# Expert rows of four graphs fetched together, x loaded twice, and upper products in pairs

## The chip, the cores and the metric

The kernel runs on one core of one Trainium2 chip. The metric is device time in microseconds (us) from start to end of the kernel, the median of three timed runs; a profiled run gives the trace beside it. The engines are TensorE (PE, with its weight loads as PEld), VectorE (DVE), ScalarE (ACT), GpSimd (POOL), and SyncE (SP), which here only issues transfers.

## The reference

There are 128 graphs of 128 nodes with 1024 features. A graph-attention layer is followed by a feed-forward layer that adds two of eight low-rank experts per graph. Cut to what matters:

```python
x = x + gnn(layernorm(x), adj, adj, W, a)       # x: (128, 128, 1024) float32
x = x + ffn(layernorm(x), router_w, lora_down, lora_up)

def gnn(h, adj, adj_weight, W, a):              # 16 heads of 64 features
    Wh = (h @ W) split into heads               # (B, 16, N, 64)
    e = leaky_relu(Wh @ a[:F] + Wh @ a[F:], 0.2)
    att = softmax(where(adj == 0, -9e15, e)) * adj_weight
    return elu(att @ Wh), heads joined again

def ffn(x, router_w, lora_down, lora_up):       # 8 experts of rank 16, top 2
    gates = softmax over the two highest of x[:, 0] @ router_w.T
    down = einsum('blh,erh->bler', x, lora_down)
    return x + einsum('bler,ehr,be->blh', down, lora_up, gates)
```

## The kernel before

The kernel walks over pairs of graphs: step q projects graphs 2q and 2q+1 with W (seven products, after Strassen's scheme, of 16 matmuls each), while attention, normalisation and the experts of earlier graphs are placed in the gaps between the products. `gaps[k]` holds what is emitted ahead of product k; every engine works through its own instructions in the order in which they are emitted. A group g is four graphs, two pairs. Its experts are chosen and their rows fetched in step 2g+2 (called an even step below) and used in step 2g+3 (an odd step). `fetch` gathers the down rows with eight indirect transfers that GpSimd issues; `fetch_up` gathers, for one graph, the 128 rows of the two chosen upper matrices (512 KB). The pool `work` has two buffers per tag unless `bufs` says otherwise; `ps_m` has four PSUM buffers of one bank.

The parts that the change and the prediction touch:

```python
    def load_x(q):
        for i in (2 * q, 2 * q + 1):
            X[i] = work.tile([P, D], F32, tag="x", name="xn", bufs=10)
            nc.sync.dma_start(X[i], x[i])

    def load_xt(q):
        XT[q] = work.tile([P, 2, KC, P], F32, tag="xt", name="xt")
        for t in range(2):
            nc.sync.dma_start(XT[q][:, t], x_t[2 * q + t])
# ... cut ...
    def stats(i, mv):

        st = small.tile([P, NH, 6], F32, tag="stats", name="stats")
        for h in range(NH):
            nc.vector.bn_stats(st[:, h, :], X[i][:, h * HALF:(h + 1) * HALF])
        nc.vector.bn_aggr(mv[:, i % 2], st)
# ... cut ...
    def pair_sums(q):

        xt = XT[q]
        a11, a12 = xt[:, 0, 0:KH], xt[:, 0, KH:KC]
        a21, a22 = xt[:, 1, 0:KH], xt[:, 1, KH:KC]
        s1, s2, s4 = (work.tile([P, KH, P], F32, tag=n, name=n, bufs=b)
                      for n, b in (("s1", 1), ("s2", 1), ("s4", 2)))
        nc.gpsimd.tensor_tensor(s1, a21, a22, ALU.add)
        nc.gpsimd.tensor_tensor(s2, s1, a11, ALU.subtract)
        s3 = a21 if q else first_s3
        nc.gpsimd.tensor_tensor(s3, a11, a21, ALU.subtract)
        nc.gpsimd.tensor_tensor(s4, a12, s2, ALU.subtract)
        SUMS[q] = (s1, s2, s3, s4)
# ... cut ...
# project(q), after setup: seven products of 16 matmuls; `bank()` gives 2 PSUM banks, two such buffers
        def product(dst, first, lhs, rhs, half_way=None):
            order = [(j, k) for j in range(2) for k in range(KH)]
            if q == 0:
                order.sort(key=lambda at: at[1])
            for at, (j, k) in enumerate(order):
                if half_way and at == KH:
                    half_way()
                nc.tensor.matmul(dst[:, j, cols], lhs[:, k, :], w_sb[:, rhs, k, j, cols],
                                 start=(first and k == 0), stop=(k == KH - 1),
                                 skip_group_check=not first)

        def read(dst, src, plus):
            nc.vector.tensor_tensor(dst[:, :, cols], src[:, :, cols], plus[:, :, cols], ALU.add)
# ... cut ...
        for step in ((product_1, product_6, product_2, product_5, product_7, product_3, product_4)
                     if q else
                     (product_1, product_2, product_7, product_6, product_5, product_3, product_4)):
            step()
            yield
# ... cut ...
    def update(i):


        att = ATT[i // 2]
        xt = X[i]
        hp = work.tile([P, D], F32, tag="hp", name="hp")
        for h, ph in enumerate(PH.pop(i)):
            nc.vector.tensor_tensor(
                hp[:, h * HALF:(h + 1) * HALF].rearrange("p (h f) -> p h f", f=F),
                ph.rearrange("p (h f) -> p h f", f=F),
                att[:, i % 2, h * HPH:(h + 1) * HPH, None].to_broadcast([P, HPH, F]),
                ALU.mult,
            )
        ex = work.tile([P, D], F32, tag="ex", name="ex", bufs=1)
        nc.scalar.activation(ex, hp, AF.Exp)
        nc.vector.scalar_tensor_tensor(xt, hp, 0.0, xt, op0=ALU.max, op1=ALU.add)
        q, t = divmod(i, 2)
        if t == 0:

            ACC[q] = small.tile([P, 3, 2], F32, tag="acc", name="acc", bufs=2)
        acc = ACC[q][:, :, t:t + 1]
        nc.vector.scalar_tensor_tensor(xt, ex, 1.0, xt, op0=ALU.min, op1=ALU.add,
                                       accum_out=acc[:, 0])
        nc.gpsimd.tensor_scalar(acc[:, 1], acc[:, 0], -1.0 / D, None, op0=ALU.mult)

    def squares(i):

        acc, t = ACC[i // 2], i % 2
        unread = scratch if i < 2 else work.tile([P, D], F8, tag="dn", name="unread", bufs=1)
        nc.scalar.activation(unread, X[i], AF.Square, bias=acc[:, 1, t:t + 1],
                             accum_out=acc[:, 2, t:t + 1], saturate=None if i < 2 else False)
# ... cut ...
    def join(i):

        g, t = divmod(i, G)
        nc.scalar.activation(X[i], X[i], AF.Identity, bias=GRP[g]["off"][:, t:t + 1],
                             scale=GRP[g]["mul"][:, t:t + 1])
# ... cut ...
        at_up = st["at_up"] = small.tile([P, G], U32, tag="at_up", name="at_up", bufs=2)
        nc.vector.tensor_scalar(at_up, of_slot, float(-R), up_row, op0=ALU.mult, op1=ALU.add)
        st["down"] = work.tile([P, G * TOP * R, KC], F32, tag="down", name="down", bufs=1)
        for j in range(G * TOP):
            nc.gpsimd.indirect_dma_start(
                out=st["down"][:, j * R:(j + 1) * R].rearrange("p r k -> p (r k)"), out_offset=None, in_=table,
                in_offset=bass.IndirectOffsetOnAxis(ap=at_down[:, j:j + 1], axis=0))

    def fetch_up(g, t):

        st = GRP[g]
        st["up", t] = work.tile([P, D], F32R, tag="up", name="up")
        nc.gpsimd.indirect_dma_start(
            out=st["up", t].bitcast(F32), out_offset=None, in_=up_table,
            in_offset=bass.IndirectOffsetOnAxis(ap=st["at_up"][:, t:t + 1], axis=0))
# ... cut ...
    def ffn_down(g):

        st = GRP[g]
        pd = ps_m.tile([P, HALF], F32, tag="pm", name="pd")
        # ... 64 matmuls into pd ...
        dn = st["dn"] = work.tile([P, G + 2, P], F32R, tag="ex", name="dn", bufs=1)
        whole = dn[:, G:G + 2]
        nc.scalar.mul(whole[:, 0], pd[:, 0:P], st["gate"])
        nc.vector.scalar_tensor_tensor(whole[:, 1], pd[:, 0:P], st["gate"],
                                       whole[:, 0].bitcast(F32), op0=ALU.mult, op1=ALU.subtract)
        for t in range(G):
            for s in range(G):
                (nc.vector.tensor_copy if s // 2 else nc.scalar.copy)(
                    dn[s * GR:(s + 1) * GR, t], whole[t * GR:(t + 1) * GR, s // 2])

    def ffn_up(g, t):

        st = GRP[g]
        st["pu", t] = [ps_m.tile([P, HALF], F32, tag="pm", name="pu") for _ in range(NH)]
        for h, pu in enumerate(st["pu", t]):
            nc.tensor.matmul(pu, st["dn"][:, t], st["up", t][:, h * HALF:(h + 1) * HALF],
                             start=True, stop=True)

    def add_up(g, t):

        st = GRP[g]
        y = X.pop(g * G + t)
        for h, pu in enumerate(st.pop(("pu", t))):
            cols = slice(h * HALF, (h + 1) * HALF)
            nc.vector.scalar_tensor_tensor(y[:, cols], pu, st["rstd"][:, t:t + 1], y[:, cols],
                                           op0=ALU.mult, op1=ALU.add)
        nc.sync.dma_start(out[g * G + t], y)
# ... cut ...
    NQ = B // 2


    for q in range(NQ + 2):
        gaps = [[] for _ in range(8)]
    # ...
        if ffn and not part:
            gaps[6] += [(logits, g), (choose, g)]
            if g < NG - 1:
                gaps[6] += [(fetch, g), (fetch_up, g, 0), (fetch_up, g, 1)]
        if q < NQ:
            gaps[6] += [(high, q, 3), (high, q, 1)]
            gaps[7].append((high, q, 2))
        # ...
        if 0 < q <= NQ:
            i = 2 * q - 2
            gaps[0].append((attention_weights, q - 1))
            if q > 3 and q % 2 == 0:
                gaps[0] += [(add_up, (q - 4) // 2, 2), (add_up, (q - 4) // 2, 3)]
            gaps[1] += [(attend, i), (update, i)]
            gaps[2].append((attend, i + 1))
            if q < NQ:
                gaps[2] += [(turn, i), (update, i + 1), (squares, i)]
                gaps[3].append((turn, i + 1))
                gaps[4 if ffn and part else 3] += [(squares, i + 1), (second_stats, q - 1)]
                gaps[4].append((rejoin, i))
                gaps[5].append((rejoin, i + 1))
            else:
                gaps[2] += [(squares, i), (update, i + 1), (turn_at_end, i),
                            (keep_turned, i)]
        # ... (last step cut)
            gaps[5 if q < NQ else 7] += [(join, i), (join, i + 1)]
            if i < B - G:
                gaps[1].append((first_row, i))
                gaps[2].append((first_row, i + 1))
        if q + 1 < NQ:
            if q:
                gaps[3].append((first_stats, 2 * q + 2))
            gaps[4 if q and not part else 5].append((pair_sums, q + 1))
            if q:
                gaps[4].append((first_stats, 2 * q + 3))
        # ...
        elif ffn and part:
            gaps[0].append((weigh, g))
            gaps[4].insert(0, (ffn_down, g))
            gaps[5][0:0] = [(ffn_up, g, 0), (ffn_up, g, 1), (add_up, g, 0), (add_up, g, 1),
                            (fetch_up, g, 2), (fetch_up, g, 3)]
            gaps[7] += [(ffn_up, g, 2), (ffn_up, g, 3)]
        # ...
        if q < NQ:
            if q:
                gaps[3].insert(0, (low, q, 0))
            gaps[6 if q else 7] += [(low, q, 3), (low, q, 1)]

        if q + 1 < NQ:
            load_xt(q + 1)
            load_x(q + 1)
        # ...
        products = project(q) if q < NQ else iter(())
        for gap in gaps:
            for f, *args in gap:
                f(*args)
            next(products, None)
```

## Time and profile before

| | before |
|---|---|
| median of three timed runs | 2036.71 us (2035.92 to 2037.42) |
| span of the profiled run | 2057.4 us |
| mean granted PE clock | 0.96 |
| moved by DMA | 380.77 MB, mean 185 GB/s |
| `x` loads | 128 of 512 KB |
| gathers of down rows, of up rows | 248 and 124 |

A line of a view names the line of the kernel, the engine, the operation and the tiles, written tile first and read tiles after the arrow. "Busy" on PE is modelled from pipelined matmuls, so the time that a product takes is read from one start to the next. The granted clock is the share of full speed that the clock of PE was allowed in a stretch.

### The profile page before, as it was taken

What the parts mean: (1) busy time and instruction counts of PE and PEld (TensorE: products, weight loads), DVE (VectorE), ACT (ScalarE), POOL (GpSimd) and SP (SyncE); (2) the same over time, 40 slices, a digit from 0 to 9 for tenths busy, and PEclk for the clock granted to TensorE, in tenths of its full rate; (3) what the DMA queues carried; (4) which work ended last, traced back from release to release, by engine and by line L of the source; (5) the groups of instructions that cost most, each with busy time, mean ns of one, the idle gap of its engine ahead of it and who ended that gap; (6) DMA issues with size and microseconds to landing.
All of it is one profiled execution on the core that took longest, in us unless ns stands there. A gap on an engine that the chain in (4) does not pass through costs nothing.

```text
span 2057.4 us, 29877 instructions
## 1 busy us (share of the span) xinstructions
PE 1937.1 (94%) x10182; PEld 1624.6 (79%) x10182; DVE 1674.0 (81%) x3674; ACT 1292.9 (63%) x1564; POOL 1017.9 (49%) x1388
## 2 busy tenths in 40 slices
PE   9989999999999999999999999999999999999997
PEld 6877877777877788777788777787877788777875
DVE  6878888888887888878888888888888888788876
ACT  3765756657567567566576576675665756666655
POOL 4445544456454465544564544655445545446451
PEclk9999999999999999999999999999999999999998
DMA  8566555666556665666655556656656655566544
GB/s 331 137 196 212 146 181 185 188 205 177 168 188 172 208 196 157 185 166 212 206 172 178 183 172 211 209 144 191 194 178 205 183 165 185 171 211 209 141 146 142
DMA packets 362910, 380.77 MB, mean 185 GB/s; under 512 B 280716, under 2 KB 282892, under 8 KB 362248
## 3 DMA queue, kind: packets, MB, share of 16 engines
q1 hardware_dynamic: 327176, 287.63, 44.9%
q0 software_dynamic: 30400, 89.68, 14.3%
q10 hardware_dynamic: 5184, 1.57, 0.3%
q8 instruction: 81, 1.33, 0.3%
q14 instruction: 69, 0.57, 0.1%
HBM read 243.52 MB, written 69.22 MB: 152 GB/s over the span
## 4 chain that ended last, share of the span: by engine, by line
PE 42%; POOL 16%; DVE 15%; ACT 10%; DMA 9%; issue 8%; DVEq 0%; SPq 0%; POOLq 0%; ACTq 0%
PE pw L472 36%; POOL down L812 10%; DMA up<-up_table,at_up 6%; POOL up L820 4%; PE ph L586 3%; ACT unread L618 3%; DMA down<-table,at_down 3%; DVE wh L477 3%; DVE parts L542 2%; DVE stats L369 2%; ACT y_t L656 2%; DVE dn L844 2%; PE pu L852 2%; ACT dn L844 1%; ACT xn L676 1%
## 5 line engine op out<-in xcount | busy, mean ns | idle before, releaser
L472 PE MATMUL pw<-w_sb,xt 128*128 128x260 f32 (+1 forms) x4080 | 988.0, 399 | 1.0 <-issue 0.8
L472 PEld LDWEIGHTS pw<-w_sb,xt 128*128 128x128 f32 x4080 | 808.2, 199 | 144.2 <-issue 8.2
L472 PE MATMUL pw<-w_sb,s 128*128 128x260 f32 (+1 forms) x3072 | 704.6, 382 | 0.0
L472 PEld LDWEIGHTS pw<-w_sb,s 128*128 128x128 f32 x3072 | 583.0, 190 | 94.3 <-DVE wh L477 0.9
L656 ACT COPY y_t<-tt 128x2048 uint16<-128x2048 uint16 x126 | 309.9, 2492 | 30.8 <-DMA tt<-halves 30.8
L650 ACT COPY halves<-xn 128x2048 uint16<-128x2048 uint16 x126 | 239.9, 1904 | 95.9 <-DVE xn L610 95.9
L812 POOL DMA_INDIRECT down<-table,at_down x248 | 258.5, 1042 | 78.8 <-issue 63.1
L612 POOL TENSOR_SCALAR acc<-acc 128x1 f32<-128x1 f32 x128 | 38.9, 305 | 490.6 <-DVE xn L610 488.2
L542 DVE SCALAR_TENSOR_TENSOR parts<-wh,rstd,parts 128x512 fp32r<-128x512 f32 x192 | 179.4, 961 | 101.7 <-ACT parts L538 101.7
L538 ACT ACTIVATE parts<-wh,rstd 128x512 fp32r<-128x512 f32 x192 | 130.8, 714 | 171.7 <-DVE wh L477 171.7
L603 ACT ACTIVATE ex<-hp 128x1024 f32<-128x1024 f32 x128 | 135.5, 1058 | 140.8 <-DVE hp L596 136.8
L596 DVE TENSOR_TENSOR hp<-ph,att 128x512 f32<-128x512 f32 x256 | 163.9, 682 | 44.2 <-PE ph L586 43.9
L852 PE MATMUL pu<-up,dn 128*128 128x512 f32 x248 | 97.1, 497 | 106.6 <-DMA up<-up_table,at_up 88.6
L630 POOL TENSOR_SCALAR rstd<-acc 128x2 f32<-128x2 f32 x64 | 12.3, 193 | 346.5 <-ACT unread L618 343.5
L618 ACT ACTIVATE unread<-xn,acc 128x1024 fp8e4<-128x1024 f32 x126 | 144.5, 1147 | 53.1 <-POOL acc L612 52.3
L477 DVE TENSOR_TENSOR wh<-pw,p 128x520 f32<-128x520 f32 (+1 forms) x192 | 132.0, 688 | 49.2 <-PE pw L472 46.6
L586 PE MATMUL ph<-parts,adj_f 128*128 128x512 f32 x512 | 165.4, 446 | 4.8 <-DVE xn L861 4.8
L861 DVE SCALAR_TENSOR_TENSOR xn<-pu,rstd,xn 128x512 f32<-128x512 f32 x248 | 168.5, 741 | 0.0
L610 DVE SCALAR_TENSOR_TENSOR xn<-ex,xn 128x1024 f32<-128x1024 f32 x128 | 156.8, 1225 | 13.7 <-ACT ex L603 0.2
L604 DVE SCALAR_TENSOR_TENSOR xn<-hp,xn 128x1024 f32<-128x1024 f32 x128 | 156.8, 1225 | 4.4
L369 DVE BATCH_NORM_STATS2 stats<-xn 128x6 f32<-128x512 f32 x248 | 158.6, 681 | 0.4
L820 POOL DMA_INDIRECT up<-up_table,at_up x124 | 140.5, 1133 | 36.2 <-issue 35.9
(183 smaller groups left out, 1975.8 us busy)
## 6 DMA issues: line engine op xcount, KB each, us to landing
xn<-in_x SPq DMA_DIRECT2D x128, 512.0 KB
xt<-in_x_t SPq DMA_DIRECT2D x127, 512.0 KB
out_y<-xn SPq DMA_DIRECT2D x124, 512.0 KB
adj_f<-in_adj_t POOLq DMA_DIRECT2D x32, 256.0 KB, 3.1
adj_i<-in_adj SPq DMA_DIRECT2D x32, 256.0 KB
down<-table,at_down POOLq DMA_INDIRECT x248, 4.5
w_sb<-in_w SPq DMA_DIRECT2D x3, 1040.0 KB
wt_sb<-in_w_t SPq DMA_DIRECT2D x1, 2048.0 KB
```

Of the source, the lines that this page charges most:

```text
L369: nc.vector.bn_stats(st[:, h, :], X[i][:, h * HALF:(h + 1) * HALF])
L472: nc.tensor.matmul(dst[:, j, cols], lhs[:, k, :], w_sb[:, rhs, k, j, cols], start=(first and k == 0), stop=(k == KH - 1), skip_group_check ...
L477: nc.vector.tensor_tensor(dst[:, :, cols], src[:, :, cols], plus[:, :, cols], ALU.add)
L542: nc.vector.scalar_tensor_tensor(in_two(PARTS[q][:, 1, b]), block, rstd, in_two(PARTS[q][:, 0, b].bitcast(F32)), op0=ALU.mult, op1=ALU.sub ...
L586: nc.tensor.matmul(PH[i][h], GRP[g]["adj_f"][:, t, :], PARTS[q][:, s, NH * (i % 2) + h], start=(s == 0), stop=(s == 1))
L596: nc.vector.tensor_tensor(hp[:, h * HALF:(h + 1) * HALF].rearrange("p (h f) -> p h f", f=F), ph.rearrange("p (h f) -> p h f", f=F), att[:, ...
L618: nc.scalar.activation(unread, X[i], AF.Square, bias=acc[:, 1, t:t + 1], accum_out=acc[:, 2, t:t + 1], saturate=None if i < 2 else False)
L650: nc.scalar.copy(halves, X[i].bitcast(U16).rearrange("p (d s) -> p s d", s=2))
L656: nc.scalar.copy(y_of(i).bitcast(U16).rearrange("p k (n s) -> p s k n", s=2), TT.pop(i).rearrange("p (s k) n -> p s k n", s=2))
L812: nc.gpsimd.indirect_dma_start(out=st["down"][:, j * R:(j + 1) * R].rearrange("p r k -> p (r k)"), out_offset=None, in_=table, in_offset=b ...
L820: nc.gpsimd.indirect_dma_start(out=st["up", t].bitcast(F32), out_offset=None, in_=up_table, in_offset=bass.IndirectOffsetOnAxis(ap=st["at_ ...
L861: nc.vector.scalar_tensor_tensor(y[:, cols], pu, st["rstd"][:, t:t + 1], y[:, cols], op0=ALU.mult, op1=ALU.add)
```

## The change

All four upper gathers of a group are issued in the even step, straight after the eight of the down rows, and land in four buffers of tag `up` where two served before. The room comes from `x`: where a tile of x stayed in SBUF from the statistics (one step ahead) until the expert's output was added, in ten buffers, it is now loaded into one of two buffers of tag `rows` for the statistics and again, late in the step before it is needed, into one of six buffers for the sum. The second pair's upper products and additions follow the first pair's by one product in the same step, where they came at the step's end and in the next step. The joins, which multiply and add the residual on ACT, move to gap 1 of the next step. The small `acc` of each graph moves from GpSimd to DVE. In odd steps the pair sums on GpSimd come one gap earlier and the second statistics one gap later. The aim is that PE doesn't wait for upper rows and that GpSimd's run of gathers holds nobody up.

The diff, with the hunks that only move buffers of the start or rename a list left out:

```diff
--- before.py
+++ after.py
# ... cut ...
@@ -98,9 +98,16 @@
         return t.rearrange("p (j c) -> p j c", j=2)
 
     def load_x(q):
+
         for i in (2 * q, 2 * q + 1):
-            X[i] = work.tile([P, D], F32, tag="x", name="xn", bufs=10)
+            X[i] = work.tile([P, D], F32, tag="x", name="xn", bufs=6)
             nc.sync.dma_start(X[i], x[i])
+
+    def load_rows(q):
+
+        for i in (2 * q, 2 * q + 1):
+            ROWS[i] = work.tile([P, D], F32, tag="rows", name="rows")
+            nc.sync.dma_start(ROWS[i], x[i])
 
     def load_xt(q):
         XT[q] = work.tile([P, 2, KC, P], F32, tag="xt", name="xt")
# ... cut ...
@@ -366,7 +374,7 @@
 
         st = small.tile([P, NH, 6], F32, tag="stats", name="stats")
         for h in range(NH):
-            nc.vector.bn_stats(st[:, h, :], X[i][:, h * HALF:(h + 1) * HALF])
+            nc.vector.bn_stats(st[:, h, :], ROWS[i][:, h * HALF:(h + 1) * HALF])
         nc.vector.bn_aggr(mv[:, i % 2], st)
 
     def rstd_of(dst, var):
@@ -390,7 +398,7 @@
         mv = MV[q][:, t]
         for h in range(NH):
             nc.scalar.activation(scratch[:, h * HALF:(h + 1) * HALF],
-                                 X[i][:, h * HALF:(h + 1) * HALF], AF.Identity,
+                                 ROWS[i][:, h * HALF:(h + 1) * HALF], AF.Identity,
                                  accum_out=mv[:, h:h + 1])
         nc.gpsimd.tensor_tensor(mv[:, 2:3], mv[:, 0:1], mv[:, 1:2], ALU.add)
         nc.gpsimd.tensor_scalar(mv[:, 3:4], mv[:, 2:3], -1.0 / D, None, op0=ALU.mult)
@@ -405,7 +413,7 @@
 
         for t in range(2):
             mv = MV[q][:, t]
-            nc.scalar.activation(scratch, X[2 * q + t], AF.Square, bias=mv[:, 3:4],
+            nc.scalar.activation(scratch, ROWS[2 * q + t], AF.Square, bias=mv[:, 3:4],
                                  accum_out=mv[:, 4:5])
         RSTD[q] = small.tile([P, 2], F32, tag="rstd", name="rstd")
         nc.gpsimd.tensor_scalar(RSTD[q], MV.pop(q)[:, :, 4], 1.0 / D, EPS, op0=ALU.mult,
@@ -609,7 +617,7 @@
         acc = ACC[q][:, :, t:t + 1]
         nc.vector.scalar_tensor_tensor(xt, ex, 1.0, xt, op0=ALU.min, op1=ALU.add,
                                        accum_out=acc[:, 0])
-        nc.gpsimd.tensor_scalar(acc[:, 1], acc[:, 0], -1.0 / D, None, op0=ALU.mult)
+        nc.vector.tensor_scalar(acc[:, 1], acc[:, 0], -1.0 / D, None, op0=ALU.mult)
 
     def squares(i):
 
@@ -805,7 +813,7 @@
         nc.vector.tensor_tensor(mine, chosen, of_two[:, None].to_broadcast([P, G, TOP]), ALU.mult)
         of_slot = small.tile([P, G], F32, tag="of_slot", name="of_slot", bufs=1)
         nc.vector.tensor_reduce(of_slot, mine, AX.X, ALU.add)
-        at_up = st["at_up"] = small.tile([P, G], U32, tag="at_up", name="at_up", bufs=2)
+        at_up = small.tile([P, G], U32, tag="at_up", name="at_up", bufs=2)
         nc.vector.tensor_scalar(at_up, of_slot, float(-R), up_row, op0=ALU.mult, op1=ALU.add)
         st["down"] = work.tile([P, G * TOP * R, KC], F32, tag="down", name="down", bufs=1)
         for j in range(G * TOP):
@@ -813,13 +821,11 @@
                 out=st["down"][:, j * R:(j + 1) * R].rearrange("p r k -> p (r k)"), out_offset=None, in_=table,
                 in_offset=bass.IndirectOffsetOnAxis(ap=at_down[:, j:j + 1], axis=0))
 
-    def fetch_up(g, t):
-
-        st = GRP[g]
-        st["up", t] = work.tile([P, D], F32R, tag="up", name="up")
-        nc.gpsimd.indirect_dma_start(
-            out=st["up", t].bitcast(F32), out_offset=None, in_=up_table,
-            in_offset=bass.IndirectOffsetOnAxis(ap=st["at_up"][:, t:t + 1], axis=0))
+        for t in range(G):
+            st["up", t] = work.tile([P, D], F32R, tag="up", name="up", bufs=4)
+            nc.gpsimd.indirect_dma_start(
+                out=st["up", t].bitcast(F32), out_offset=None, in_=up_table,
+                in_offset=bass.IndirectOffsetOnAxis(ap=at_up[:, t:t + 1], axis=0))
 
     def ffn_down(g):
 
@@ -974,7 +980,7 @@
         if ffn and not part:
             gaps[6] += [(logits, g), (choose, g)]
             if g < NG - 1:
-                gaps[6] += [(fetch, g), (fetch_up, g, 0), (fetch_up, g, 1)]
+                gaps[6].append((fetch, g))
         if q < NQ:
             gaps[6] += [(high, q, 3), (high, q, 1)]
             gaps[7].append((high, q, 2))
@@ -985,14 +991,15 @@
         if 0 < q <= NQ:
             i = 2 * q - 2
             gaps[0].append((attention_weights, q - 1))
-            if q > 3 and q % 2 == 0:
-                gaps[0] += [(add_up, (q - 4) // 2, 2), (add_up, (q - 4) // 2, 3)]
+            if q > 1:
+                gaps[1] += [(join, i - 2), (join, i - 1)]
             gaps[1] += [(attend, i), (update, i)]
             gaps[2].append((attend, i + 1))
             if q < NQ:
                 gaps[2] += [(turn, i), (update, i + 1), (squares, i)]
                 gaps[3].append((turn, i + 1))
-                gaps[4 if ffn and part else 3] += [(squares, i + 1), (second_stats, q - 1)]
+                gaps[4 if ffn and part else 3].append((squares, i + 1))
+                gaps[5 if ffn and part else 3].append((second_stats, q - 1))
                 gaps[4].append((rejoin, i))
                 gaps[5].append((rejoin, i + 1))
             else:
@@ -1001,14 +1008,15 @@
                 gaps[3] += [(squares, i + 1), (turned_parts, NG - 1, False),
                             (turn_at_end, i + 1), (stay_busy, 1, ident), (turned_parts, NG - 1, True),
                             (keep_turned, i + 1), (second_stats, q - 1)]
-            gaps[5 if q < NQ else 7] += [(join, i), (join, i + 1)]
+            if q == NQ:
+                gaps[7] += [(join, i), (join, i + 1)]
             if i < B - G:
                 gaps[1].append((first_row, i))
                 gaps[2].append((first_row, i + 1))
         if q + 1 < NQ:
             if q:
                 gaps[3].append((first_stats, 2 * q + 2))
-            gaps[4 if q and not part else 5].append((pair_sums, q + 1))
+            gaps[4 if q else 5].append((pair_sums, q + 1))
             if q:
                 gaps[4].append((first_stats, 2 * q + 3))
         if ffn and not part:
@@ -1027,9 +1035,8 @@
         elif ffn and part:
             gaps[0].append((weigh, g))
             gaps[4].insert(0, (ffn_down, g))
-            gaps[5][0:0] = [(ffn_up, g, 0), (ffn_up, g, 1), (add_up, g, 0), (add_up, g, 1),
-                            (fetch_up, g, 2), (fetch_up, g, 3)]
-            gaps[7] += [(ffn_up, g, 2), (ffn_up, g, 3)]
+            gaps[5][0:0] = [(ffn_up, g, 0), (ffn_up, g, 1), (add_up, g, 0), (add_up, g, 1)]
+            gaps[6] += [(ffn_up, g, 2), (ffn_up, g, 3), (add_up, g, 2), (add_up, g, 3)]
         if q % 2 == 0 and q < NQ:
             gaps[5].append((group_adj, q // 2))
             if q // 2 + 1 < NG:
@@ -1041,7 +1048,9 @@
 
         if q + 1 < NQ:
             load_xt(q + 1)
-            load_x(q + 1)
+            load_rows(q + 1)
+        if 0 < q < NQ:
+            gaps[6].insert(0, (load_x, q))
         if q == 0:
             gaps[7] += [(sums_of, 2), (sums_of, 3), (load_up,)]
         if q == 1:
```

## The prediction

> **What bounds the kernel now.** I began with the page: busy shares, then the chain that ended last.
>
> ```profile
> PE 1937.1 (94%) x10182; PEld 1624.6 (79%) x10182; DVE 1674.0 (81%) x3674; ACT 1292.9 (63%) x1564; POOL 1017.9 (49%) x1388
> ```
>
> TensorE (PE) is nearly full, so the question is where its missing 6% sits, and whether its "busy" time is all useful. The list of waits, for all engines (us in total, times, longest), answers the first:
>
> ```profile
> ACT parts L538 <- DVE wh L477: 171.7, 64, 3.9
> ...
> PE pu L852 <- DMA up<-up_table,at_up: 88.6, 49, 3.9
> ...
> ACT unread L618 <- POOL acc L612: 52.3, 33, 2.6
> ```
>
> PE has practically one wait, at the upper products of line 852, for the rows being fetched (88.6 us; with other releasers the group's idle time is 106.6 us). The timeline of PE through the end of an odd step shows the pattern:
>
> ```profile
> 945.75 3.67 PE L472 MATMUL pw<-w_sb,s 128*128 128x260 f32 x16
> 949.25 3.67 PE L472 MATMUL pw<-w_sb,xt 128*128 128x260 f32 x16
> 954.56 0.69 PE L852 MATMUL pu<-up,dn 128*128 128x512 f32 x2 [1.64 <-DMA up<-up_table,at_up]
> 956.28 0.71 PE L852 MATMUL pu<-up,dn 128*128 128x512 f32 x2 [1.03 <-DMA up<-up_table,at_up]
> 956.83 5.35 PE L472 MATMUL pw<-w_sb,xt 128*128 128x260 f32 x16
> 961.83 1.28 PE L586 MATMUL ph<-parts,adj_f 128*128 128x512 f32 x4
> ```
>
> Read the starts, not the durations. A product of 16 matmuls takes 949.25 - 945.75 = 3.50 us. The second one should end at 952.75, and four pu matmuls should take 1.12 us (as the first four, 944.63 to 945.75), so the next product should start at 953.87; it starts at 956.83, 2.96 us late. That product then takes 961.83 - 956.83 = 5.00 us where its like in undisturbed steps takes about 3.4: another 1.6. The granted clock in 4 us windows says why (the columns are PE, PEld, DVE, ACT, POOL, then the clock, the DMA share and GB/s):
>
> ```profile
> 948.00:952.00 4.00, 4.00 (x20) 3.48 (x19) 2.16 (x4) 4.00 (x4) 3.51 (x4) 1.00 0.62 188
> 952.00:956.00 4.00, 1.61 (x7) 0.75 (x5) 2.66 (x2) 1.92 (x3) 3.92 (x4) 1.00 1.03 378
> 956.00:960.00 4.00, 3.71 (x11) 3.01 (x12) 3.76 (x14) 0.98 (x2) 1.23 (x1) 0.66 0.99 394
> 960.00:964.00 4.00, 4.00 (x18) 3.35 (x17) 3.69 (x6) 0.59 (x1) 0.00 (x0) 0.91 0.72 297
> ```
>
> The pause costs a second time, by a cold clock. The whole loss is 4.6 us here, 4.7 in the next group; the rest of the group is an unbroken stream of PE work. From 961.83 to the same place in the next group, 1023.78, is 61.95 us; without the loss it is 57.3.
>
> Why the rows are late is in the chain that ended last, in order of time (start, us):
>
> ```profile
> 934.58 0.95 POOL up L820
> ...
> 935.83 1.52 POOL up L820
> ...
> 937.43 0.54 POOL acc L612
> 937.99 1.24 ACT unread L618 x2
> 939.23 0.58 ACT parts L538
> ```
>
> GpSimd (POOL) issues ten gathers in a row, about 1.0 us each and 0.30 us apart, so the small `acc` of line 612 waits behind them, ScalarE (ACT) waits for `acc`, and VectorE (DVE) for ACT. The last two gathers need the two `up` buffers back from the first upper products (945.75); they issue at 948.84 and 950.22 and take a median 6.1 us to land, while PE is ready for them at 952.75.
>
> **What the Trainium skill says.** "TensorE: Matmul & The Clock Gate", Part 1: The HAM clock gate, gives half rate after an idle window of about 3.4 us and full rate only after a busy one. The trace agrees: clock 0.66 in the window after the pause, and 5.00 us for a product. "SBUF — State Buffer", Who interferes with whom: a DVE instruction with two SBUF inputs, or a copy or cast in a two-port mode, shares a port pair with GpSimd, and the second to issue is blocked until the first ends. The trace agrees; the timelines of POOL and of DVE in an even step show it:
>
> ```profile
> 915.28 1.26 POOL L422 TENSOR_TENSOR s<-xt 128x512 f32<-128x512 f32 x1
> ```
> ```profile
> 915.72 0.87 DVE L709 TENSOR_TENSOR add<-of_graph,part 128x32 f32<-128x32 f32 x1
> ```
>
> An operation on 32 elements, which elsewhere takes 0.19 us, ends just as the POOL one does. "DMA: Bandwidth & Descriptors", SWDGE vs HWDGE vs iDMA, says that an engine takes turns between the queues of GpSimd and of SP; this trace does not test it.
>
> **The change part by part.** (1) Gathers of rows 3 and 4 move from the odd step to the even one. Twelve in a row: from 923.82, eight of 1.04 + 0.30 and four of 1.13 + 0.30 make 16.4 us at most, so the last issues at about 939 and lands about 945; needed at 949.25 (the second pair now in gap 6). Their wait goes, and with it the cold product: 31 groups by 4.7 = 145 us, all on the path that sets the end. (2) `acc` on DVE: 128 small instructions at about 0.15 us (the tiny ones of lines 771 and 772), 19 us, 0.6 per group, in exchange for 52.3 us of ACT waiting; beside PE, so it gains nothing by itself but brings ACT's read of product 2 forward by some 1.5 us. (3) Joins, two per step at 1.23 us, go from gap 5 to gap 1 of the next step, where ACT was idle 2.98 us before `ex`; they may delay `ex` by about 0.7. The 2.36 us before lines 538 and 542 in the odd step goes (DVE stood 3.17 us there). (4) x twice: 2.1 MB per group, at the 394 GB/s of a full window 5.4 us of DMA time; DMA goes from 0.60 x 62 = 37 us to 42.6 us of about 58, or 74%. (5) The second x load waits until the first pair's output has left: about 951 to 953, landed by 957, needed about 959.5. It holds, with some 2 us to spare. (6) The upper products of the second pair come one product, not two, after the first, and need the four PSUM buffers that four additions of 0.74 us must free. (7) Pair sums in odd steps move a gap earlier: POOL is then at 5.5 us of additions from about 939.3 to 944.8, just when DVE makes its eight casts into `dn`. These run 0.22 us for 128 elements against 0.19 for 32, so I take them for a two-port mode: each can be blocked by up to 1.3 us. I expect `dn` 1 to 2 us later (0.5 us of waiting at the first pu), then additions ending about 951 with the second pair wanted at 949.9 (0.5 us more). Estimate: 0.8 us x 31 = 25 us given back. These pauses are too short to cool the clock.
>
> Sum in the profile: 2057.4 - 145 = 1912 as floor, +25 = 1937. The timed runs are at 2036.7 while the profiled run took 2059.6. If profiling stretches everything alike, the timed floor is 1912 x 2036.7 / 2059.6 = 1891; if it only lengthens the wait (matmuls should run at their rate either way), it stays 1912. I take the middle, 1902, and add 25: about 1928.
>
> **Rivals.** DVE becomes the bound: it is busy 50.7 us per 62, so 51.3 of 57.3, 90%. For: it is 3 us behind PE in even steps already (`hp` at 929.59 for products begun at 926.63). Against: it still has pauses, 2.03 us at line 542 for ACT, which part 2 shortens. If it bound, gaps would spread: about 1960. The transfers become the bound: twelve gathers, two transposes and the step's loads crowd into 923 to 948, where the share is already 0.85 to 1.02. If transposes land late, ACT's `y_t` waits grow from 30.8 us, and DVE follows: 1950 to 1980. The new x load takes the place of the old wait, if outputs leave late: 2 us and a cold product again, near 2000. Best case, no contention at the casts: 1895 to 1905.
>
> **Range and chances.** 1900 to 1968 covers floor by either reading and all but the last rival. For under 2% the group must keep over 70% of its loss (4.7 less 40.7 / 31 = 1.3 us): faster 0.94, same 0.05, slower 0.01.
>
> **What would show it.** Right: PE's wait for `up` under 10 us, clock 0.99 or 1.00 in the middle windows, period about 58, POOL no longer releasing line 618. Part 7: the DVE casts of line 844 well over 0.22 us, small waits of PE at line 852 for `dn` or line 861. Wrong: PE waiting for `xn` of line 604 or 610 or its DMA, `y_t` waits well over 60 us, or a clock still near 0.96.

## The result, and the profile after

| | before | after |
|---|---|---|
| median of the timed runs | 2037.07 us (2035.92 to 2039.98) | 1982.12 us (1979.68 to 1983.08) |
| span of the profiled run | 2057.4 us | 1980.3 us |
| mean granted PE clock | 0.96 | 0.997 |
| mean period of a group in the trace | 63.1 us | 60.6 us |
| moved by DMA | 380.77 MB | 446.87 MB |

The ratio is 0.9726, 95% interval 0.9709 to 0.9743. The gain is 55 us where 109 were predicted, and the time lies above the predicted range. The period is read from one start of the down products to the next, over 30 groups. The difference, 2.5 us by 30, makes up 75 of the 77 us between the two spans, so the steady groups hold the answer.

The busy shares of the changed kernel, and the first line of its chain that ended last:

```profile
PE 1907.6 (96%) x10182; PEld 1590.9 (80%) x10182; DVE 1689.8 (85%) x3802; ACT 1294.6 (65%) x1564; POOL 944.1 (48%) x1260
...
PE 86%; DVE 5%; issue 3%; DMA 3%; POOL 2%; ACT 1%; another core or an unknown queue 0%; SPq 0%; DVEq 0%; ACTq 0%
```

The chain now runs through PE for 86% of the span, where POOL, DVE, ACT and DMA had half of it before:

```profile
PE 42%; POOL 16%; DVE 15%; ACT 10%; DMA 9%; issue 8%; DVEq 0%; SPq 0%; POOLq 0%; ACTq 0%
```

PE still lacks 4%. Its list of waits (us in total, times, longest) says where:

```profile
PE pd L836 <- issue: 41.9, 57, 1.9
PE pu L858 <- DMA up<-up_table,at_up: 6.3, 3, 3.2
```

The wait for upper rows is down from 88.6 to 6.3 us, as intended. In its place stands a wait that the kernel before did not have, at the down products, with "issue" as releaser: PE waited for nothing that the profile shows. PE's timeline through the end of an odd step of the changed kernel:

```profile
1019.40 3.67 PE L480 MATMUL pw<-w_sb,s 128*128 128x260 f32 x16
1023.00 0.44 PE L836 MATMUL pd<-y_t,down 128*32 128x128 f32 x4
1024.58 0.27 PE L836 MATMUL pd<-y_t,down 128*32 128x128 f32 x1 [1.13 <-issue]
1025.30 1.97 PE L836 MATMUL pd<-y_t,down 128*32 128x128 f32 x59 [0.46 <-issue]
1027.20 3.77 PE L480 MATMUL pw<-w_sb,xt 128*128 128x260 f32 x16
...
1035.25 0.97 PE L858 MATMUL pu<-up,dn 128*128 128x512 f32 x2
1036.43 1.11 PE L858 MATMUL pu<-up,dn 128*128 128x512 f32 x2 [0.21 <-issue]
1037.38 7.17 PE L480 MATMUL pw<-w_sb,xt 128*128 128x260 f32 x32
```

The 64 down products take 4.20 us to the next product (1023.00 to 1027.20). In the kernel before they ran without a gap (939.29 to 941.21, 1.92 us to the next product):

```profile
939.29 1.99 PE L830 MATMUL pd<-y_t,down 128*32 128x128 f32 x64
941.21 3.77 PE L472 MATMUL pw<-w_sb,xt 128*128 128x260 f32 x16
```

From the first start to the last, the trace has 1.71 us in every group before and 3.0 to 4.3 after; the excess over all 31 groups is 65 us, 2.1 per group. The second pair's four upper products take 2.13 us to the next product, which is also the median of 30 groups; a block that nothing holds up took 1.12 (944.63 to 945.75 before). What GpSimd and DVE do meanwhile, in their timelines of the same group:

```profile
1020.84 1.65 POOL L826 DMA_INDIRECT up<-up_table,at_up  x1 [0.30 <-issue]
1022.79 1.02 POOL L826 DMA_INDIRECT up<-up_table,at_up  x1 [0.31 <-issue]
1025.61 1.30 POOL L430 TENSOR_TENSOR s<-xt 128x512 f32<-128x512 f32 x1 [1.79 <-remote]
...
1028.22 1.28 POOL L433 TENSOR_TENSOR xt<-xt 128x512 f32<-128x512 f32 x1
1029.45 1.28 POOL L434 TENSOR_TENSOR s<-xt,s 128x512 f32<-128x512 f32 x1
```
```profile
1029.28 2.97 DVE L850 CAST dn<-dn 32x128 fp32r<-32x128 f32 x8
```

The same casts in the kernel before:

```profile
942.93 1.89 DVE L844 CAST dn<-dn 32x128 fp32r<-32x128 f32 x8
```

Two things coincide. The twelfth gather is being issued until 1023.81, 0.8 us after PE has come to the down products; with ten, the last ended some 2 us ahead of them (935.83 + 1.52 = 937.35, against 939.29). And the pair sums run while DVE makes its casts.

### The profile page after: what moved, and what is told of

The parts are those of the page before. It is cut to its first block, busy times and chain, and to the rows that moved or that the text cites. A ratio compares the mean times of both kernels' runs of the same rounds, so it can differ in the third digit from the quotient of the medians.

```text
span 1980.3 us, 30167 instructions
## 1 busy us (share of the span) xinstructions
PE 1907.6 (96%) x10182; PEld 1590.9 (80%) x10182; DVE 1689.8 (85%) x3802; ACT 1294.6 (65%) x1564; POOL 944.1 (48%) x1260
## 2 busy tenths in 40 slices
DMA packets 381058, 446.87 MB, mean 226 GB/s; under 512 B 282732, under 2 KB 284908, under 8 KB 380392
## 4 chain that ended last, share of the span: by engine, by line
PE 86%; DVE 5%; issue 3%; DMA 3%; POOL 2%; ACT 1%; another core or an unknown queue 0%; SPq 0%; DVEq 0%; ACTq 0%
PE pw L480 73%; PE ph L594 5%; PE pd L836 4%; PE pu L858 3%; DMA up<-up_table,at_up 2%; POOL down L820 1%; DVE xn L867 1%; DMA w_sb<-in_w 1%; DVE wh L485 1%; POOL up L826 0%; DVE parts L550 0%; PE pu L922 0%; DVE hp L604 0%; DVE xn L618 0%
## 5 line engine op out<-in xcount | busy, mean ns | idle before, releaser
L480 PE MATMUL pw<-w_sb,xt 128*128 128x260 f32 (+1 forms) x4080 | 935.5, 385 | 0.5 <-DMA w_sb<-in_w 0.5
L480 PEld LDWEIGHTS pw<-w_sb,xt 128*128 128x128 f32 x4080 | 771.7, 190 | 125.5 <-issue 7.0
L664 ACT COPY y_t<-tt 128x2048 uint16<-128x2048 uint16 x126 | 310.4, 2492 | 54.5 <-DMA tt<-halves 54.3
L546 ACT ACTIVATE parts<-wh,rstd 128x512 fp32r<-128x512 f32 x192 | 136.9, 719 | 227.9 <-DVE wh L485 227.9
L618 DVE SCALAR_TENSOR_TENSOR xn<-ex,xn 128x1024 f32<-128x1024 f32 x128 | 156.8, 1225 | 34.7 <-ACT ex L611 24.6
L377 DVE BATCH_NORM_STATS2 stats<-rows 128x6 f32<-128x512 f32 x248 | 158.6, 681 | 0.4
L826 POOL DMA_INDIRECT up<-up_table,at_up x124 | 135.1, 1089 | 37.8 <-issue 37.2
L684 ACT ACTIVATE xn<-xn,off,mul 128x1024 f32<-128x1024 f32 x128 | 151.8, 1235 | 0.0
L550 DVE SCALAR_TENSOR_TENSOR parts<-wh,rstd,parts 128x512 fp32r<-128x512 f32 x192 | 137.7, 743 | 6.9 <-ACT parts L546 6.8
L836 PE MATMUL pd<-y_t,down 128*32 128x128 f32 x1984 | 84.2, 277 | 42.0 <-issue 41.9
```

Of the source, the lines that this page charges most:

```text
L377: nc.vector.bn_stats(st[:, h, :], ROWS[i][:, h * HALF:(h + 1) * HALF])
L664: nc.scalar.copy(y_of(i).bitcast(U16).rearrange("p k (n s) -> p s k n", s=2), TT.pop(i).rearrange("p (s k) n -> p s k n", s=2))
L836: nc.tensor.matmul(pd[t * GR:(t + 1) * GR, 0:P], st["down"][:, t * GR:(t + 1) * GR, k], st["y_t"][:, k, t * P:(t + 1) * P], start=(k == 0) ...
```

## The experiments

Two theories compete for the down products. **G**: gathers that GpSimd issues as PE comes to them slow PE. **X**: the added load of x, and its traffic, does it. A further question is what the blocked casts cost. The runs used three chips, on which the kernel before took 2042 (e1 to e4), 2062 to 2063 (e5 to e8, e16, e17) and 2047 to 2067 us (e9 to e15), so only runs of one chip, or ratios to the kernel before, are compared. Of each edit the lines that matter are shown. The last column is the time from the first to the last start of the 64 down products, over the first 30 of the 31 groups, worked out from the traces; the last group is told of below the table.

| run | time | ratio to before, 95% interval | down products, us |
|---|---|---|---|
| e1 before, unchanged | 2043.67 | 0.9998 [0.9977, 1.0019] | 1.71 |
| e2 after, two gathers emitted later | 1982.57 | 0.9700 [0.9657, 0.9743] | 3.2 to 5.9 |
| e3 after, second x load cut to 1/16 | 1982.66 | 0.9704 [0.9661, 0.9747] | 3.2 to 4.9 |
| e4 after, pair sums late | 1984.48 | 0.9741 [0.9679, 0.9802] | 3.3 to 5.0 |
| e5 after, two gathers split off | 2002.50 | 0.9698 [0.9663, 0.9732] | 1.71 |
| e6 as e5, other pair sums late | 1913.11 | 0.9262 [0.9208, 0.9316] | 1.71 |
| e7 before, `acc` on DVE | 2006.55 | 0.9730 [0.9703, 0.9756] | 1.71 |
| e8 as e7, three more gathers | 2105.21 | 1.0198 [1.0168, 1.0227] | 4.1 to 6.8 |
| e9 after, again | 1971.47 | 0.9541 [0.9524, 0.9557] | 2.8 to 4.0 |
| e10 e6 again | 1940.16 | 0.9413 [0.9363, 0.9463] | 1.71 |
| e11 after, `acc` on GpSimd | 1968.28 | 0.9526 [0.9510, 0.9542] | 2.6 to 4.1 |
| e12 as e7, GpSimd busy instead | 2019.63 | 0.9868 [0.9820, 0.9916] | 1.71 |
| e13 as e7, three gathers elsewhere | 2017.66 | 0.9864 [0.9816, 0.9911] | 1.71 to 1.74 |
| e14 e7 again | 2013.01 | 0.9843 [0.9788, 0.9898] | 1.71 to 1.80 |
| e15 e8 again | 2126.17 | 1.0382 [1.0328, 1.0437] | 4.9 to 7.2 |
| e16 as e6, one gather split off | 1970.74 | 0.9564 [0.9505, 0.9624] | 1.71 |
| e17 e6 again | 1912.48 | 0.9298 [0.9248, 0.9347] | 1.71 |

The 1913.11 of e6 is the median of three runs; a fourth, 1941.62 at a clock of 0.989, was over 1.5% above the fastest and is left out as disturbed.

The last group of e5, e6, e10, e16 and e17 has no pair sum to hold the late gathers back, so twelve are issued in a row there, the last one until 0.8 us after the first down product in all five. The down products took 2.75, 2.87 and 3.52 us in e5, e6 and e10, but 1.71 in e16 and e17. The part on what stays open comes back to this.

**e1, the kernel before.** Unchanged.

> The kernel before, unchanged, so that its trace comes from the same chip as the others. If the slow start of the down products (their 64 matmuls take 3.0 to 4.3 us from first to last start in the changed kernel, 1.7 us in the trace of the kernel before) belongs to the change, this shows 1.7 us again in every group, PE's semaphore updates on time, and 2035 to 2040 us. If it belongs to the chip or to the way the trace was taken, it shows 3 us or more here too.

It repeats the time of before, and 1.71 us in every group: the slow start belongs to the changed kernel.

**e2, the last two gathers emitted behind the down products.**

```diff
-            gaps[4].insert(0, (ffn_down, g))
+            gaps[4][0:0] = [(ffn_down, g), (fetch_up, g, range(2, 4))]
```

> The changed kernel with its third and fourth gather of upper rows issued in the odd step, just behind the down products, still into four buffers: ten gathers in a row, as before the change. Theory G (the row of twelve gathers, which still runs when PE comes to the down products, slows PE's sequencer there): the down products take 1.7 us again, 65 us go, about 1920 us. Theory X (the second load of x and the traffic it adds): nothing of that moves, 1975 to 1990 us. In both, the late rows must still be there for the second pair: issued about 1026 and 1027 on the clock of the changed kernel's trace, landing about 1033, needed at 1035.

It did not test what it meant to. GpSimd had nothing else to do, so it ran ahead and issued twelve in a row again, from 1014.26 to beyond 1028.71 in one group. The time is that of the changed kernel. Emitting the two gathers behind a PE instruction did not delay them, since GpSimd waited for nothing of PE's there. In two groups of e2 the twelfth gather had ended 0.07 and 0.19 us before the down products began, and they still took 3.2 and 3.3 us.

**e3, the second load of x cut to 64 of its 1024 columns**, into six fixed buffers. The residual sum is left on old contents, so the output is not the reference's.

```diff
-            X[i] = work.tile([P, D], F32, tag="x", name="xn", bufs=6)
-            nc.sync.dma_start(X[i], x[i])
+            X[i] = xbuf[i % 6]
+            nc.sync.dma_start(X[i][:, 0:F], x[i, :, 0:F])
```

> The changed kernel, where the second load of x fetches 64 of 1024 columns only (the sum is then taken over old contents, the work is the same): the traffic that the change added is nearly gone, all instructions stay. Theory X: the down products take 1.7 us, about 1920 us. Theory G: they stay above 3 us and the time is 1970 to 1985 us.

The time did not move, and the wait stayed; from the waits of PE in e3:

```profile
PE pd L840 <- issue: 41.5, 58, 1.9
```

X falls: with 1/16 of the second load nothing changes that these runs can measure.

**e4, pair sums of odd steps back in gap 5.**

```diff
-            gaps[4 if q else 5].append((pair_sums, q + 1))
+            gaps[4 if q and not part else 5].append((pair_sums, q + 1))
```

> The changed kernel with the pair sums of odd steps back in gap 5, behind the eight casts into dn. If the casts are held up by GpSimd's additions, they take 1.9 us again instead of 3.7, the wait of 0.7 us inside the second block of upper products goes, and up to 20 us with it: about 1962 us. If the additions then hold up the low parts of line 550 as much, nothing is gained: 1975 to 1990 us. The down products keep their 3 to 4 us in both.

The casts are free again, in the timeline of DVE in e4:

```profile
731.09 1.89 DVE L850 CAST dn<-dn 32x128 fp32r<-32x128 f32 x8
...
740.88 2.66 DVE L550 SCALAR_TENSOR_TENSOR parts<-wh,rstd,parts 128x512 fp32r<-128x512 f32 x2
```

The second pair's upper products were down to 1.26 us, so the blocked casts were what made them late. But the pair sums now fall on line 550 (2.66 us for two, 0.74 each elsewhere), PE waited 24.0 us for upper rows where it had waited 6.3, and nothing was won. The slow start stayed, so the casts are not its cause.

**e5, the last two gathers put behind the first pair sum**, which overwrites `s1`, a buffer that PE's product ahead of the down products reads, and so can't run ahead.

```diff
         nc.gpsimd.tensor_tensor(s1, a21, a22, ALU.add)
+        if between is not None:
+            fetch_up(between, range(2, 4))
```

> In e2 the two late gathers found GpSimd free and followed the other ten at once, so the row of twelve was not broken. Here they stand behind the first of the pair sums, which waits for PE to finish the product ahead of the down products: ten gathers in a row, ending some 2 us before the down products, then the last two from about 1.5 to 4 us after their start. Theory G (gathers being issued while PE comes to the down products slow its sequencer): the down products take 1.7 to 2 us again and 55 to 65 us go: 1915 to 1930 us. If the slow start has another cause (where the products wait, or the semaphores that the gathers share), it stays at 3 us or more, and the time at 1975 to 1990 us.

The down products are back at 1.71 us in all groups but the last: G stands. Yet the ratio to the kernel before, 0.9698, is that of e2 to e4 (the changed kernel itself was not run on this chip; elsewhere it had 0.9541 and 0.9726), because the other three pair sums, pushed behind the gathers, now cover all the casts. Timelines of DVE and of PE in e5:

```profile
973.90 5.57 DVE L865 CAST dn<-dn 32x128 fp32r<-32x128 f32 x8
```
```profile
970.16 1.99 PE L851 MATMUL pd<-y_t,down 128*32 128x128 f32 x64
972.08 3.77 PE L489 MATMUL pw<-w_sb,xt 128*128 128x260 f32 x16
978.14 2.05 PE L873 MATMUL pu<-up,dn 128*128 128x512 f32 x4 [2.29 <-ACT unread L635]
```

Eight casts take 5.57 us; the first alone lasts from 973.90 to 977.80, held by three additions in a row. PE pauses 2.29 us for `dn`; such pauses add up to 64.1 us in 28 of this run's waits. The ScalarE operation that the view names as releaser had ended at 977.27; the second cast, which completes the first graph's `dn`, ended at 978.03 and PE began at 978.14. The product after it takes 3.97 us (979.98 to 983.95) for about 3.3: the granted clock was 0.50 from 978 to 980 and 0.68 from 980 to 982. "SBUF — State Buffer", Who interferes with whom, in the Trainium skill says that of DVE and GpSimd on their shared ports the one that issues first holds the other for the whole instruction; 1.89, 2.97 and 5.57 us for the same eight casts, with none, some and most of the additions beside them, agree that the casts are held. Which issued first these traces don't show: the first cast is recorded from 973.90, the addition that held it from 974.00.

**e6, as e5, with the other three pair sums behind the second statistics, in gap 5.**

```diff
-            gaps[4 if q else 5].append((pair_sums, q + 1, g if ffn and part else None))
+            gaps[4 if q else 5].append((pair_sums, q + 1, g if ffn and part else None,
+                                        gaps[5] if ffn and part else None))
```

> As e5, and the other three pair sums of odd steps moved behind the second statistics, out of the way of the eight casts into dn. Under theory G the down products take 1.7 to 2 us; the casts take 1.9 us instead of 3.7 and the second block of upper products 1.1 to 1.3 us instead of 1.8: up to 20 us better than e5. If the low parts of line 550 lose what the casts gain, the same as e5.

1913.11 us, below both kernels. PE's timeline in e6 has no gap:

```profile
932.11 1.98 PE L851 MATMUL pd<-y_t,down 128*32 128x128 f32 x64
934.02 3.77 PE L489 MATMUL pw<-w_sb,xt 128*128 128x260 f32 x16
937.44 1.28 PE L873 MATMUL pu<-up,dn 128*128 128x512 f32 x4
938.56 3.67 PE L489 MATMUL pw<-w_sb,s 128*128 128x260 f32 x16
941.88 1.28 PE L873 MATMUL pu<-up,dn 128*128 128x512 f32 x4
```

Either cure alone (e4, e5) left the ratio to the kernel before where it was; both together brought 89 us over e5.

**e7, the kernel before with `acc` on DVE, and e8, the same with three more gathers** of 64 bytes per row behind the ten, which nobody reads.

```diff
-        nc.gpsimd.tensor_scalar(acc[:, 1], acc[:, 0], -1.0 / D, None, op0=ALU.mult)
+        nc.vector.tensor_scalar(acc[:, 1], acc[:, 0], -1.0 / D, None, op0=ALU.mult)
```
```diff
-                gaps[6] += [(fetch, g), (fetch_up, g, 0), (fetch_up, g, 1)]
+                gaps[6] += [(fetch, g), (fetch_up, g, 0), (fetch_up, g, 1), (fetch_more, g)]
```

> The kernel before with nothing changed but acc on DVE. ACT then doesn't wait for GpSimd's row of gathers, the second statistics come some 1.5 us earlier and so do the third and fourth gather of upper rows, for which PE waits 2.9 us a group. If the row of gathers is what makes the rows late: 2.9 shrinks to about 1.4 us, the clock stays up in many groups, and 45 to 95 us go: 1940 to 1990 us. If the two buffers are (free at the first upper products, whatever GpSimd does): under 20 us go, 2015 to 2040 us. The down products keep 1.7 us.

> The kernel of e7 with three more gathers of 64 bytes a row, which nobody reads, behind the ten: GpSimd issues until about 2 us after the start of the down products, while nothing else of the change is there. Theory G: the down products take 3 us or more, as in the changed kernel. The time may stay that of e7, because a PE that comes later waits less for its upper rows. If they take 1.7 us, theory G falls.

e8 is 98.7 us above e7, and the slow start appears in the kernel before, without a second load of x or four buffers. Its down products are even slower, and the gathers end later, 1.5 to 3.7 us after PE has come to them. `acc` by itself brought 2.7% (57 us, within the 45 to 95 named), though PE's wait for upper rows only fell to 60.6 us, from 88.6 before and 74.7 in e1.

**e9 to e11, on one chip: after again, e6 again, and after with `acc` back on GpSimd.**

> The changed kernel itself, unchanged, beside the next two on one chip. Both theories: 1980 to 1985 us where the kernel before takes 2037 to 2042; where the kernel before takes 2060, up to 2005. The 64 down products of a group start over 3 to 4.5 us in most groups.

> The kernel of the split gathers and moved pair sums once more, on the chip of the changed kernel. Theory of the gathers (twelve in a row keep GpSimd issuing into the down products, and the pair sums hold the casts): 60 to 75 us below the changed kernel. Rival (the 1916 us of its first run owed something to that chip): less than 40 us below it. The 64 down products start over 1.7 us in all groups.

> The changed kernel with the small acc operation put back on GpSimd, behind the twelve gathers. If its move to DVE is a part the gain can't do without: acc waits until the twelfth gather is issued, the second half of parts and the unread operation of ScalarE wait for it, and the time is 2020 to 2060 us with GpSimd as releaser of ScalarE's unread line again. If the joined gathers bring the gain by themselves: within 10 us of the changed kernel.

On this chip e6 is 31 us below the changed kernel. By the words on record that is the rival's side: part of what e6 gained on its first chip was not there. It is not the down products (1.71 us); PE's wait for upper rows was 33.2 us in e10, 20.0 in e6 and 13.7 in e17, and 7.7 in the changed kernel of e9. The two late gathers are the weak place of that version. The `acc` operation, worth 1.6 to 2.7% in the kernel before (e14, e7), is worth nothing in the changed one (1968.28 without its move, 1971.47 with it, intervals overlapping).

**e12 to e15, on one chip: what about the gathers it is.** e12 puts six small operations in place of the three unread gathers, e13 issues the gathers behind the pair sums; e14 and e15 repeat e7 and e8.

```diff
-                gaps[6] += [(fetch, g), (fetch_up, g, 0), (fetch_up, g, 1), (fetch_more, g)]
+                gaps[6] += [(fetch, g), (fetch_up, g, 0), (fetch_up, g, 1), (busy_more,)]
```
```diff
+            if ffn and part:
+                gaps[5].append((fetch_more, g))
```

> The kernel before with acc on DVE, and behind the ten gathers six small arithmetic operations on GpSimd (some 4 us) in place of three more gathers. Theory of the gathers being issued: as the kernel with acc alone on the same chip within 15 us, and the down products start over 1.7 us. Rival (any work on GpSimd at that place): 60 to 100 us above it, and 4 us or more.

> The kernel before with acc on DVE, and the three unread gathers issued behind the pair sums, some 20 us after the down products. Theory of the gathers being issued while PE comes to the down products: at most 30 us above the kernel with acc alone (they may hold GpSimd's next small operations), and the down products start over 1.7 us. Rival (three more gathers in a group, wherever): 60 to 100 us above it.

> The kernel before with acc on DVE once more, for the same chip: 2.5 to 3.5% below the kernel before, down products over 1.7 us.

> The same with three unread gathers behind the ten, once more for the same chip: 80 to 110 us above the kernel with acc alone, down products over 4 to 6 us.

e14 is 1.6% below the kernel before, where 2.5 to 3.5 were expected. e14 to e15 is 113 us, a little over the 80 to 110 expected. Of these, busy GpSimd at the same place costs 7 (e12), and the same gathers elsewhere cost 5 (e13), both within the intervals. GpSimd and PE in e12:

```profile
975.35 0.95 POOL L820 DMA_INDIRECT up<-up_table,at_up  x1 [0.30 <-issue]
976.37 0.47 POOL L827 TENSOR_SCALAR more<-half_pow 128x2 f32<-128x2 f32 x1
976.93 4.86 POOL L829 TENSOR_TENSOR more<-more,half_pow 128x2 f32<-128x2 f32 x5
```
```profile
978.78 1.98 PE L837 MATMUL pd<-y_t,down 128*32 128x128 f32 x64
```

and PE in e15:

```profile
968.68 0.44 PE L839 MATMUL pd<-y_t,down 128*32 128x128 f32 x4
969.46 0.27 PE L839 MATMUL pd<-y_t,down 128*32 128x128 f32 x1 [0.33 <-issue]
970.19 0.31 PE L839 MATMUL pd<-y_t,down 128*32 128x128 f32 x1 [0.46 <-issue]
...
971.60 0.32 PE L839 MATMUL pd<-y_t,down 128*32 128x128 f32 x1 [0.38 <-issue]
972.29 3.26 PE L839 MATMUL pd<-y_t,down 128*32 128x128 f32 x56 [0.38 <-issue]
```

GpSimd computes straight through the down products in e12 and they keep their 1.71 us. In e15 single matmuls come 0.7 us apart. It takes more gathers, at that place.

**e16, as e6 with eleven gathers in a row and one behind the pair sum; e17, e6 once more beside it.**

```diff
-        fetch_up(g, range(2))
+        fetch_up(g, range(3))
```

> As the kernel of the split gathers with moved pair sums, but eleven gathers in a row and one behind the pair sum. The eleventh ends about the time the down products start. If only gathers issued after their start hurt: they start over 1.7 us, PE's wait for upper rows falls by half, and the time is 5 to 15 us below the kernel with two late gathers. If a gather just ahead of them hurts too: 2.5 us or more, and the time is 15 to 40 us above it.

> The kernel of the split gathers and moved pair sums, for the same chip: 0.92 to 0.945 of the kernel before.

Half right. The down products keep their 1.71 us, although in six of thirty groups the eleventh gather is still being issued as they start; the timelines of GpSimd and of PE in one of them:

```profile
179.51 0.93 POOL L841 DMA_INDIRECT up<-up_table,at_up  x1 [0.30 <-issue]
```
```profile
179.96 1.99 PE L851 MATMUL pd<-y_t,down 128*32 128x128 f32 x64
```

This can't be set against the changed kernel, though: in the traces of e16 and e17 even twelve in a row, in the last group, do no harm. The wait for upper rows did not halve; from the waits of PE in e16 and in e17:

```profile
PE pu L873 <- DMA up<-up_table,at_up: 59.0, 21, 7.7
```
```profile
PE pu L873 <- DMA up<-up_table,at_up: 13.7, 14, 4.8
```

The single late gather kept PE waiting for up to 7.7 us, the clock was 0.985 (0.996 in e17), and e16 is 58 us above e17. Why one late transfer lands later than two was not found.

## Why the prediction was wrong

The direction was right and the gain was half. The failed step is the "0.8 us x 31 = 25 us given back". An unbroken group takes 57.3 us by the prediction's own reading, so the changed kernel, at 60.6, loses 3.3 us per group, 102 us in all, for 25.

- **The missing term, 2.1 of the 3.3 us: the down products' slow start.** Part 1 placed the last issue at about 939 and asked only whether the rows would be there at 949.25. The same group had its down products at 939.29. That GpSimd would still be issuing gathers as PE came to them stood in these numbers, and the cost of it was in none of the prediction's lists of waits, because behind ten gathers the down products had always kept their 1.71 us. e5 takes the slow start away by breaking the row, e8 and e15 bring it about in the kernel before by lengthening the row, and e12 and e13 show that neither arithmetic there nor gathers elsewhere do it.
- **Part 7, right in kind.** The casts were blocked as foretold (eight took 2.95 to 4.01 us, for 1.89, in all groups but one). From the product behind the down products to the end of the second pair's block PE took 10.17 us in the changed kernel and 8.97 in e17 (medians of 30 groups): 1.2 us more where 0.8 had been taken, 1.0 of it at the second pair's block (2.13 against 1.12). With the 2.1 this makes the 3.3.
- **The floor was off in the other direction.** "The whole loss is 4.6 us here, 4.7 in the next group" was read from two groups. The mean period before is 63.1, a loss of 5.8 us, so the floor is 2057.4 - 31 x 5.8 = 1878, 34 us below the 1912 taken. The sum then closes: 1937 - 34 + 77 = 1980, the span of the profile. The two errors hid each other in part, so a nearer hit would have been partly luck.
- **Between profile and timed runs** the prediction took the middle, 10 us off the profile's reading. The timed runs after, 1982.12, agree with the profiled one, 1982.15. So do those of the kernel before in e1 (2043.67, profiled 2044.03), with all its pauses; the 23 us between the timed runs and the profile of before belonged to that one recording, and why is not known.
- **Part 1's gain** came: the wait for upper rows fell to 6.3 us (under 10 was said) and the clock rose to 0.997. The prediction found the trace in agreement with the idle window of about 3.4 us that it cites for the cold clock. The half rate is there (0.50 for 3.41 us in e5), but not an idle time of that length: the pauses around it were of 1.64 and 1.03 us in the kernel before and of 2.29 us in e5.
- **Part 2** was to gain nothing by itself. In the changed kernel that holds (e11). In the kernel before it brought 1.6 to 2.7%. Why PE's loss per group falls with it there, while the third gather of upper rows is issued only 0.2 us earlier after the start of the down products (medians 9.34 us in e7, 9.55 before), was not followed up. The prediction read the two buffers, free at 945.75, as what this gather waits for; in the same trace GpSimd works through seven small operations of the statistics from 945.80 to 948.67 first.
- **Part 3** held in size: DVE waits for the delayed `ex` 31 times, 24.6 us or 0.8 each against the 0.7 foretold, without PE waiting for it. **Parts 4 and 5** held: e3 cuts the second load to 1/16 and moves nothing. **Part 6** held, with part 7's delay.
- **The rivals.** Neither DVE (85% busy) nor the transfers became the bound, although the time fell near the figures given for them: ACT's waits for transposes rose from 30.8 to 54.3 us, under the 60 named as a sign, and e6 has the same transfers and a period of 57.0 to 57.6 us in undisturbed groups. A range that ended at 1968 left no room for a cost that none of the rivals named.

**What stays open.** That two or three more gathers in the row ahead of the down products slow PE's stream is shown; how, is not. Nor is the exact condition. In the changed kernel, e2, e3, e4 and e11 there are groups in which the last of twelve gathers ended up to 0.6 us before the down products started, and they took 3.2 to 3.5 us all the same, while behind ten gathers that ended 0.4 us before their start or 0.1 us after it (e7) they took 1.71. So the length of the row may count, and not only what is being issued at that moment.

The last group makes it less certain still. e10 and e17 are the same kernel, and GpSimd issues its last gather there at the same time against the down products. The last gather on GpSimd and the first of the down products, in e10 and then in e17:

```profile
1884.98 0.94 POOL L841 DMA_INDIRECT up<-up_table,at_up  x1 [0.31 <-issue]
1885.11 1.03 PE L851 MATMUL pd<-y_t,down 128*32 128x128 f32 x10
```
```profile
1852.73 0.93 POOL L841 DMA_INDIRECT up<-up_table,at_up  x1 [0.30 <-issue]
1852.87 1.98 PE L851 MATMUL pd<-y_t,down 128*32 128x128 f32 x64
```

In e10 the starts spread over 3.52 us, in e17 over 1.71. One thing that differs is the record: in the traces of before, e16 and e17 the gathers have times of landing and no wait ends at "remote" (a releaser that the trace doesn't tell), and in all the others it is the other way round. The changed kernel and e8 were never recorded in the fuller way, so whether they would be slow there is untested. What the timed runs do say is that three more gathers cost 98.7 and 113 us (e8, e15), about the 109 and 128 us by which the starts of their down products are stretched in the traces.

A rival that the trace can settle is a shortage of instructions, as the page lists two DMA queues of kind "instruction" (81 and 73 packets in the changed kernel). In 26 of the 31 groups no packet of these queues moves from 1 us ahead of the first down product to the last, and these groups took 3.3 to 4.3 us like the others, so PE was not waiting for such a packet.

In the changed kernel's trace other engines too see PE's releases late around the down products (from the list of waits for all engines):

```profile
ACT parts L546 <- remote: 61.5, 26, 3.7
...
POOL s L430 <- remote: 46.8, 25, 2.4
```

This points at the signals between engines rather than at the data, which e8 and e15 also suggest, as their added gathers move only 8 KB each (128 rows of 64 bytes). It is a pointer and no more: e6, without the slow start in all but its last group, has 45 us of such waits too, of 130 in the changed kernel. Every run here was made with a recorded clock and span, so whether the recording has a share in the effect can't be told.

## What to carry to other kernels

Moving a transfer's issue earlier costs more than buffers: look at what the other engines start while GpSimd issues a long run of gathers, and end the run well before PE comes to a block of small matmuls (2 us before was enough here), or break it with an instruction that has to wait for PE (e5). Place GpSimd's additions away from DVE's casts. When two losses lie behind each other, curing one can show nothing (e4, e5); try both before a cause is dismissed. And take a loss per group from the mean of all periods, not from two groups that are easy to read.

## What the runs showed of the hardware that had not been expected

- Two or three more indirect gathers in the row that GpSimd issues just ahead of 64 small matmuls of PE stretch the starts of these from 1.71 to between 2.6 and 7.2 us, although the matmuls read nothing of the added gathers (e8, e15, and the changed kernel); six arithmetic operations on GpSimd at the same place do not. "SBUF — State Buffer", Who interferes with whom, says "PE and ACT never wait on anyone." It speaks of SBUF ports, and e12 agrees with that; what slows PE beside the gathers is not known.
- The effect does not hang on the row alone: twelve gathers, the last issued until 0.8 us after the start of the matmuls, went with 3.52 us in one run of a kernel and with 1.71 in another (last groups of e10 and e17).
- Eight casts of 32x128 on DVE grew from 1.89 to 5.57 us beside three additions on GpSimd (e5).
- Medians of one and the same kernel differ between occasions by more than the runs of one occasion do: 2037 to 2067 us for the kernel before, 1971 and 1982 for the changed one, 1912 to 1940 for the kernel of e6. The ratios 0.9541 and 0.9726 of the same change differ for that reason.
